# Convolution with residual: the eight VectorE residuals in the middle go the way of the others, and three of four images are combined from image 130

## The chip, the cores and the metric

The kernel runs on one core of one Trainium2 chip. The metric is the device time of one execution in microseconds (us); the median of several executions is compared. TensorE (PE in the profile, its weight loads PEld), VectorE (DVE), ScalarE (ACT), GpSimd (POOL) and SyncE (SP, which issues DMAs) each run their own instructions in order, and wait for each other by semaphores.

## The reference, cut to what matters

```python
# x: (160, 128, 32, 32) f32;  U: (5, 128*128*9) f32
def _gn(v, G=32, eps=1e-5):                  # groups of 4 channels
    g = v.reshape(B_, G, C_ // G, H_, W_)
    m = jnp.mean(g, axis=(2, 3, 4), keepdims=True)
    s = jnp.var(g, axis=(2, 3, 4), keepdims=True)
    return ((g - m) / jnp.sqrt(s + eps)).reshape(v.shape)

s1 = (max(U) - min(U)) / 3.0                 # weights in two quantised parts
v1 = s1 * floor(U / s1)
s2 = s1 / 5.0
v2 = s2 * floor((U - v1) / s2)
w = (v1 + v2).reshape(OUT_CH * 5, IN_CH, 3, 3)
# images 0, 5, 10, ... use weight set 0; 1, 6, 11, ... use set 1; and so on
act = conv(x.reshape(B // 5, 5 * C, H, W), w, padding 1, feature_group_count=5)
out = x + act(_gn(x))                        # the residual
```

Every image is normalised, convolved 3 by 3 with one of five weight sets, and added to its own input.

## The kernel before, in words

The kernel orders the images by weight set: image i of the loop is number `i % 32` of set `i // 32`. One image is a tile of 128 channels by 1024 pixels. Images are loaded in chunks of two (1 MB) into 12 chunk buffers (`CHUNKS`). The order of all instructions is written out by hand in `run` (line 971): iteration i of its loop convolves image i and prepares others at fixed distances.

In iteration i (lines 1103 to 1252), for an image beyond the start:

- **TensorE** (`conv`, 859): first the products m2 and m1 of image i+1 (`sums_of_pairs`, 851), then the main products of image i (`main`, 875) into its pair of PSUM banks, eo. There are two such pairs. The multiplication uses a high and a low f16 part of each image.
- **Two kinds of image.** A *direct* image has a high part hi (`high_part`, ScalarE, 645), a low part lo (VectorE, 748) and three row sums of lo (`combinations`, VectorE, lines 761, 769, 770); it takes 30 matmuls. A *combined* image (`combined`, 648) has its pixels combined in v before the split, by GpSimd (lines 675 and 705) and VectorE (`combine`, 687 and 694), then vh (ScalarE, 735) and vl (VectorE, 741); it takes 24 matmuls. Up to image 29 every second image is combined, then, until `THIRDS` = 146, three of five, and from there three of four.
- **VectorE** in its order: vl or lo and rows of image i+2; a residual by VectorE, if image i-1 has one; eo of image i+1 from m1 and m2 (`pairs`, 897 and 899); v of image i+4 (687 and 694). Steps of the quantisation of the next weight set (lines 134 to 172, by `Later`, 37) are spread between them until four images before the set begins.
- **ScalarE** in its order: the first statistics pass of an image some 14 ahead (241), the copy of the finished image i-1 from PSUM to sum (`residual`, 923), the copy m2 of image i+1 from PSUM to SBUF (`leave`, 888), vh or hi of image i+3, the second statistics pass (248).
- **GpSimd**: the rest of a group's statistics (rstd, line 286), its part of v, or z (711) of image i+4, and an accumulating DMA (`accumulate`, 947). `beside_pairs` and `after` (698, 724) tie the first ones to a VectorE instruction, so that they start at a chosen point.

Statistics are gathered in groups of eight images from image 24 on; the first image of a group, if direct, has its z made by ScalarE (637).

**The residual** has two forms (`residual`, 915). In most images ScalarE copies eo to one of three sum buffers, and GpSimd's queue issues a DMA that adds sum to the output in DRAM (512 KB). The input has been stored there long before (`store_input`, 957), two images in one 1 MB DMA of SP's queue. For images for which `by_hand` (910) is true, VectorE adds eo to the input in its chunk (line 940, one instruction), and SP stores the result (`store`, 955); the other image of that chunk is stored alone. These are images 0 to 2, 39, 55, 71, 87, 103, 119, 135, 151 and 156 to 159.

`by_hand` also sets when a chunk is free for the next load: `consumed` (967) gives iteration i+2 for an image by hand and i-2 for the others. Loads stand in SP's queue in that order, behind the stores.

Of the kernel before, what the change touches and what calls it, by code (L numbers as in the profile page):

```python
# [22 lines left out]
LAST = 4  # L23
# [361 lines left out]
class Main:  # L385
# [27 lines left out]
    STEADY = 7  # L413
    BY_VECTOR = (8, 10, 11, 14, 19, 24, 29, 34)
    FIFTHS = 30
    THIRDS = 146
    EARLY = 8
    FIRST = 3
    HURRIED = (0, 2, 4, 8, 24)
# [228 lines left out]
    def combined(self, i):  # L648
# [4 lines left out]
        if i < self.FIFTHS:  # L653
            return i % 2 == 1
        return i % 5 % 2 == 0 if i < self.THIRDS else i % 4 != 2

# [253 lines left out]
    def by_hand(self, i):  # L910


        return i < self.FIRST or i >= self.imgs - LAST or i > self.FIFTHS and i % 16 == 7

    def residual(self, i):

# [385 lines left out]
```

## Time and profile before

| | |
|---|---|
| median of 3 executions | 975.06 us (974.68 to 976.52) |
| the profiled execution | 975.07 us, its span 973.3 us |
| granted TensorE clock | 0.996 |
| images convolved after the start | 157, from 55 us to 965 us |
| from one VectorE residual in the middle to the next (16 images) | 90 to 93 us |
| residuals by ScalarE's copy and an accumulating DMA | 145 |
| residuals by one VectorE addition of a whole image (line 940) | 13 |
| combined images | 92 |
| DMA queues, share of 16 engines over the span | SP's 46.3%, GpSimd's 42.2% |

The span lies between the first and the last instruction; the time also has what lies around it. Busy time of matmuls is not TensorE at its peak, since matmuls overlap: one follows another after some 0.21 us, although each record lasts about 0.38 us. Idle time that a view shows in brackets is that of the engine just before the instruction, with what ended it. Idle time of an engine that is not on the path costs nothing by itself.

### The profile page before, as it was taken

To read this page: it belongs to the slowest core of one execution; us is meant where nothing else is said; L and a number is where in the kernel's file an instruction comes from. 1 tells how busy PE (TensorE), PEld (TensorE's weight loads), DVE (VectorE), ACT (ScalarE), POOL (GpSimd) and SP (SyncE) were. 2 spreads that over 40 slices of the span, in tenths; PEclk is the share of its full clock that TensorE was granted. 3 is DMA by queue.
4 is the path that set the end of the run, shared out by engine and by line. 5 is a ranking of instruction groups with operands and counts; after the bars stand their busy time and mean duration, and the time that the engine had idled before them with its cause. 6 is when DMAs were issued, how large, how long until landed. Compare 5 with 4: busy or idle time off the path is not lost. (4 is left out here: it accounts for less than half of the span.)

```text
span 973.3 us, 13056 instructions
## 1 busy us (share of the span) xinstructions
PE 930.4 (96%) x4444; PEld 434.5 (45%) x4444; DVE 914.9 (94%) x1290; ACT 854.1 (88%) x1160; POOL 459.3 (47%) x466
## 2 busy tenths in 40 slices
PE   2899999999999999999999999999999999999996
PEld 1344444444444444444444444444444444444443
DVE  7989999999999999989999999999999999988994
ACT  5779999999999999999889999999989999997551
POOL 4345445446335444554355436534444565575550
PEclk9999999999999999999999999999999999999999
DMA  9079999999999997998899899979997999655553
GB/s 352 29 277 345 331 332 322 330 322 318 329 329 337 313 305 217 273 320 229 242 271 319 216 269 298 326 168 298 325 299 158 295 323 229 142 93 92 94 98 112
DMA packets 66427, 250.04 MB, mean 257 GB/s; under 512 B 5296, under 2 KB 5296, under 8 KB 66352
## 3 DMA queue, kind: packets, MB, share of 16 engines
q1 hardware_dynamic: 45472, 173.09, 46.3%
q0 software_dynamic: 20880, 76.03, 42.2%
q8 instruction: 37, 0.61, 0.2%
q14 instruction: 38, 0.31, 0.1%
HBM read 89.19 MB, written 159.91 MB: 256 GB/s over the span
## 5 line engine op out<-in xcount | busy, mean ns | idle before, releaser
L785 PE MATMUL eo<-hi,wt 128*128 128x496 f16 (+3 forms) x1206 | 320.4, 376 | 1.3 <-ACT wt L567 0.7
L840 PEld LDWEIGHTS <-wt 128*128 128x128 f16 x1884 | 183.5, 99 | 213.4 <-DVE rows L770 3.1
L741 DVE SCALAR_TENSOR_TENSOR vl<-v,rstd,vh 128x2048 f16<-128x2048 f32 x92 | 216.8, 2356 | 1.0 <-ACT vh L735 0.9
L840 PE MATMUL eo<-vh,wt 128*128 128x512 f16 x552 | 206.8, 375 | 0.4 <-DVE eo L899 0.2
L840 PE MATMUL eo<-vl,wt 128*128 128x512 f16 x552 | 206.7, 375 | 0.0
L735 ACT ACTIVATE vh<-v,rstd 128x2048 f16<-128x2048 f32 x92 | 184.2, 2002 | 20.5 <-DVE v L694 20.2
L785 PEld LDWEIGHTS <-wt 128*128 128x128 f16 x1278 | 124.7, 99 | 146.7 <-DVE eo L899 4.1
L675 POOL TENSOR_SCALAR v<-xt,ngm 128x64 f32<-128x64 f32 x92 | 85.3, 927 | 219.1 <-issue 63.3
L923 ACT COPY sum<-eo 128x1024 f32<-128x1024 f32 x145 | 152.1, 1049 | 30.6 <-PE eo L840 30.1
L248 ACT ACTIVATE junk<-xt,mv 128x1024 uint8<-128x1024 f32 x152 | 174.5, 1148 | 0.1
L241 ACT ACTIVATE junk<-xt 128x1024 uint8<-128x1024 f32 x152 | 160.5, 1056 | 13.1 <-DMA xt<-in_x_dram 10.0
L711 POOL TENSOR_SCALAR z<-xt,ngm,rstd 128x1024 f32<-128x1024 f32 x50 | 90.1, 1802 | 171.3 <-DVE rows L769 61.0
L840 PEld LDWEIGHTS <-across 128*128 128x128 f16 x1104 | 107.9, 98 | 137.5 <-issue 13.3
L840 PE MATMUL eo<-rows,wt 128*128 128x496 f16 (+1 forms) x390 | 148.1, 380 | 0.0
L947 POOL DMA_DIRECT2D out_dram<-sum x145 | 127.0, 876 | 6.9 <-ACT sum L923 5.8
L888 ACT ACTIVATE m<-m 128x512 f32<-128x512 f32 x157 | 94.0, 598 | 22.1 <-PE m L840 18.1
L840 PE MATMUL m<-vl,across 128*128 128x496 f16 (+1 forms) x276 | 103.3, 374 | 9.4 <-DVE vl L741 9.4
L687 DVE TENSOR_TENSOR v<-xt 128x960 f32<-128x960 f32 x92 | 106.4, 1157 | 0.0
L840 PE MATMUL m<-vh,across 128*128 128x496 f16 (+1 forms) x276 | 103.4, 375 | 0.9 <-ACT m L888 0.9
L705 POOL TENSOR_TENSOR v<-xt 128x512 f32<-128x512 f32 x92 | 95.3, 1036 | 0.0
L748 DVE TENSOR_TENSOR lo<-z,hi 128x1024 f16<-128x1024 f32 x68 | 83.0, 1221 | 0.0
L645 ACT CAST hi<-z 128x1024 f16<-128x1024 f32 x68 | 71.1, 1045 | 0.5
(146 smaller groups left out, 1162.3 us busy)
## 6 DMA issues: line engine op xcount, KB each, us to landing
xt<-in_x_dram SPq DMA_DIRECT2D x78, 1024.0 KB, 12.2
out_dram<-sum POOLq DMA_DIRECT2D x145, 512.0 KB, 8.7
out_dram<-xt SPq DMA_DIRECT2D x68, 1024.0 KB, 17.2
out_dram<-xt SPq DMA_DIRECT2D x23, 512.0 KB, 8.1
u<-in_L_conv_U_dram SPq DMA_DIRECT2D x4, 576.0 KB, 10.6
xt<-in_x_dram SPq DMA_DIRECT2D x4, 512.0 KB, 10.2
range<-in_L_conv_U_dram SPq DMA_DIRECT2D x3, 576.0 KB, 8.3
u<-in_L_conv_U_dram SPq DMA_DIRECT2D x2, 288.0 KB, 3.2
```

The costliest lines, as they stand in the source:

```text
L241: self.nc.scalar.activation(junk, image, ACTF.Copy, scale=-1.0 / image.shape[1], accum_out=self.mv[:, j, 0:1],)
L248: self.nc.scalar.activation(junk, image, ACTF.Square, bias=self.mv[:, j, 0:1], accum_out=self.mv[:, j, 1:2],)
L687: nc.vector.tensor_tensor(self.view(v, 1, (511, 2), (half, H), (1, half - 1)), self.view(x, 1, (1, 2), (W, H), (2, half - 1)), self.view(x ...
L705: ins = nc.gpsimd.tensor_sub(self.v[i][:, 1536:], odd, even)
L711: ins = nc.gpsimd.tensor_scalar(z, self.image(i), st.ngm[:, j], st.rstd[:, j], ALU.add, ALU.mult)
L735: self.nc.scalar.mul(vh, self.v[i], st.rstd[:, j])
L741: yield self.nc.vector.scalar_tensor_tensor(vl, self.v[i], st.rstd[:, j], self.hi[i], ALU.mult, ALU.subtract)
L785: nc.tensor.matmul(self.bank(target, a)[:, first:end, c0:c1], self.wts[n, col][:, k, :], tile[:, s0 : s0 + 2 * (end - first) - 1 : 2, c0 + ...
L840: self.nc.tensor.matmul(out, weights, moving, start=start and j == 0, stop=False, skip_group_check=True)
L888: self.nc.scalar.mul(m2, self.m2_ps, 0.5)
L923: nc.scalar.copy(self.as_banks(i, self.sum[i]), self.flat(i, eo))
L947: added = self.nc.gpsimd.dma_start(self.ov[n, :, b], self.sum.pop(i), accum_op=ALU.add)
```

## The change

`by_hand` loses its third case, so that only the first three and the last four images are added by VectorE. Images 39, 55, 71, 87, 103, 119, 135 and 151 go through ScalarE's copy and the accumulating DMA, their inputs are stored with their neighbours', and their chunks are free four iterations earlier. `THIRDS` goes from 146 to 130: of images 130 to 145, twelve are combined (all but 130, 134, 138 and 142) where ten were (130, 132, 134, 135, 137, 139, 140, 142, 144, 145).

```diff
@@ class Main
     STEADY = 7
     BY_VECTOR = (8, 10, 11, 14, 19, 24, 29, 34)
     FIFTHS = 30
-    THIRDS = 146
+    THIRDS = 130
     EARLY = 8
@@ def by_hand(self, i)
-        return i < self.FIRST or i >= self.imgs - LAST or i > self.FIFTHS and i % 16 == 7
+        return i < self.FIRST or i >= self.imgs - LAST
```

## The prediction

> **What bounds the kernel now.** I read the page first, then the busy times in stretches, then the waits of TensorE, then the timeline around each wait. The page's first part:
>
> ```profile
> PE 930.4 (96%) x4444; PEld 434.5 (45%) x4444; DVE 914.9 (94%) x1290; ACT 854.1 (88%) x1160; POOL 459.3 (47%) x466
> ```
>
> Three engines are nearly full, so the averages decide nothing. The next view has stretches that each run from one VectorE residual in the middle to the next, 16 images (columns: length, busy PE, PEld, DVE, ACT, POOL, then clock, DMA share, GB/s):
>
> ```profile
> 284.20:376.50 92.30, 92.25 (x445) 43.16 (x443) 90.74 (x128) 89.72 (x124) 41.09 (x42) 1.00 1.00 295
> 376.50:469.40 92.90, 90.91 (x434) 42.29 (x433) 88.37 (x121) 84.92 (x115) 44.01 (x44) 1.00 0.93 265
> 653.20:746.00 92.80, 89.89 (x432) 41.53 (x431) 90.56 (x123) 86.40 (x121) 42.85 (x43) 1.00 0.93 264
> 746.00:836.10 90.10, 90.10 (x434) 42.30 (x433) 83.39 (x114) 86.52 (x117) 48.40 (x42) 1.00 0.95 265
> 836.10:927.00 90.90, 89.92 (x430) 42.07 (x429) 81.98 (x101) 70.55 (x87) 52.84 (x45) 1.00 0.60 105
> ```
>
> The reader is to see that 16 images take some 90 us where TensorE never waits (746 to 836), and 92 to 93 us where VectorE also quantises the next weight set. So TensorE's own work bounds the kernel, plus the times at which VectorE is late. Those times are few after image 30, and each stands in TensorE's timeline (the bracket is idle time and its releaser):
>
> ```profile
> 383.32 0.38 PE L840 MATMUL m<-vl,across 128*128 128x512 f16 x1 [1.05 <-DVE vl L741]
> 469.30 0.38 PE L840 MATMUL m<-vl,across 128*128 128x512 f16 x1 [0.66 <-DVE vl L741]
> 472.28 0.39 PE L785 MATMUL eo<-hi,wt 128*128 128x512 f16 x1 [0.50 <-DVE eo L899]
> 500.55 0.38 PE L840 MATMUL m<-vl,across 128*128 128x512 f16 x1 [1.95 <-DVE vl L741]
> 684.23 0.60 PE L840 MATMUL m<-rows,wt 128*128 128x512 f16 x2 [0.87 <-DVE rows L770]
> 730.40 0.38 PE L840 MATMUL m<-vl,across 128*128 128x512 f16 x1 [1.95 <-DVE vl L741]
> 911.20 0.38 PE L840 MATMUL m<-vl,across 128*128 128x512 f16 x1 [0.98 <-DVE vl L741]
> 933.85 0.38 PE L840 MATMUL m<-vl,across 128*128 128x512 f16 x1 [0.87 <-DVE vl L741]
> ```
>
> Matmuls follow each other every 0.21 us although a record lasts 0.38, so a wait costs about 0.16 more than its bracket: 381.90 to 383.32 is 1.42 from start to start, 1.21 of it lost. The eight cost 8.83 + 8 x 0.16 = 10.1 us.
>
> **What the Trainium skill says.** Perfetto Trace Analysis, "Identifying the Most-Contended Engine": matmul busy time is no measure of TensorE's limit; occupancy is one for VectorE and ScalarE. The 0.38 and 0.21 agree, which is why I count starts. SBUF — State Buffer, "Who interferes with whom": a VectorE instruction with two SBUF inputs and a GpSimd instruction that reads SBUF exclude each other. The trace agrees: L309 takes 0.17 us alone and 0.96 beside L705 (906.18), L675 takes 0.4 alone and 2.3 beside a vl. The residual addition has one PSUM and one SBUF input, so removing it should free no GpSimd time. ScalarE: Activation LUTs, "What ACT_TABLE_LOAD costs": back-to-back ACTIVATEs overlap by about 93 ns; here a copy of 1.05 us holds ScalarE 0.97 from start to start (701.75 to 702.72). DMA: Bandwidth & Descriptors, "Issuing engines are not separate DMA queues": all DMAs share 16 engines, so the added accumulating stores compete with loads wherever they are issued.
>
> **The change part by part.** Costs are from these rows:
>
> ```profile
> L940 DVE TENSOR_TENSOR xt<-eo,xt 128x1024 f32<-128x1024 f32 x13 | 15.8, 1218 | 4.7 <-PE eo L840 3.6 <-PE eo L785 1.0
> L923 ACT COPY sum<-eo 128x1024 f32<-128x1024 f32 x145 | 152.1, 1049 | 30.6 <-PE eo L840 30.1
> L947 POOL DMA_DIRECT2D out_dram<-sum x145 | 127.0, 876 | 6.9 <-ACT sum L923 5.8 <-DMA out_dram<-xt 1.1
> ```
>
> *1. Eight additions leave VectorE* (images 39, 55, 71, 87, 103, 119, 135, 151). Each held it 1.35 us from its start to the next start (284.23 to 285.58): 8 x 1.35 = 10.8 us. This is worth only what a TensorE wait behind it was worth, before VectorE next has time to spare. Image by image: 39 (284.2) and 55 (376.5) precede the wait at 383.32, with VectorE never waiting between; 1.21 goes. 71 (469.4) precedes 472.28: 471.41 to 472.28 less 0.21 is 0.66, gone. The wait at 469.30 lies ahead of that addition and stays. VectorE then waits 1.02 us for ScalarE at 482.89, which uses up the rest of the lead, so 500.55 stays. 87 (562.4): VectorE waits at 600.83, 617.57 and 628.99, TensorE not until 684; nothing. 103 (653.2): no VectorE wait over 0.25 before 684.23, so that goes: 1.04. What is left of the lead ends at 712.75 (0.74 waiting for ScalarE), so 730.40 stays. 119 and 135: TensorE doesn't wait behind them; nothing. 151 (927.0): the wait at 933.85 goes, 1.04. Sum: 1.21 + 0.66 + 1.04 + 1.04 = 3.95 us.
>
> *2. Eight copies go to ScalarE*, 0.97 each, 7.8 us, ahead of the copy m2 (L888) in its queue, for which VectorE's L897 waits, and ahead of vh or hi and the second statistics pass. What hides them is the wait that ScalarE has right behind each of these images now:
>
> ```profile
> 288.83 2.00 ACT L735 ACTIVATE vh<-v,rstd 128x2048 f16<-128x2048 f32 x1 [1.35 <-DVE v L694]
> 381.11 2.00 ACT L735 ACTIVATE vh<-v,rstd 128x2048 f16<-128x2048 f32 x1 [1.58 <-DVE v L694]
> 467.08 2.00 ACT L735 ACTIVATE vh<-v,rstd 128x2048 f16<-128x2048 f32 x1 [1.21 <-DVE v L694]
> 650.85 0.60 ACT L888 ACTIVATE m<-m 128x512 f32<-128x512 f32 x1 [2.31 <-PE m L840]
> 750.64 2.00 ACT L735 ACTIVATE vh<-v,rstd 128x2048 f16<-128x2048 f32 x1 [1.27 <-DVE v L694]
> 839.46 1.02 ACT L923 COPY sum<-eo 128x1024 f32<-128x1024 f32 x1 [1.08 <-PE eo L840]
> ```
>
> Image 87 has three short ones (0.58, 0.26, 0.34 from 564.76), and 151 has 1.27 at 928.97. At 39 the copy moves m2 from 282.19 to 283.16, still ahead of VectorE, which comes to L897 at 284.23 without the addition. Where v released ScalarE, v comes 1.35 earlier as well. Cost 0; with that cover gone, 7.8.
>
> *3. DMA and queues.* Eight more accumulating stores: GpSimd 8 x 0.88 = 7 us (it is 47% busy, and the issue stands behind the work VectorE needs); on the DMA engines 42.2% x 973.3 / 145 = 2.83 us each, 23 us in all, where the shares of the page (46.3 + 42.2 + 0.4) leave 108 idle. A store lands a median 8.7 us after issue (12.4 at most), and three sum buffers last about 3 x 5.8 = 17 us, so ScalarE shouldn't wait. On SP the late store of each of these images goes; the queue stood behind it (292.3 us in 12 waits), and the chunk is freed four iterations earlier. No engine waited for a load after 80 us, so this is worth 0. Bounds: no gain, since nobody waits; at worst, landings slow enough to hold sum buffers, put at 1 us for each of the eight stores, which the range covers in part.
>
> *4. Two more combined images.* In 130 to 145 there are 12 for 10. A combined one costs TensorE 2.54 + 2.55 us (390.88 to 393.42, 379.35 to 381.90), a direct one 1.29 + 5.11 (372.70 to 379.10): 1.31 less, 2.6 for two. VectorE takes on 2 x 1.5 us and has 95.87 of 107.30 busy at 774.7 to 882.0. ScalarE, start to start: statistics 2.32, sum 0.97, m2 0.48, and vh 1.90 or hi 0.93, so 5.67 or 4.70; 12 x 5.67 + 4 x 4.70 + 0.3 = 87.1 us for 16 images, against TensorE's 12 x 5.09 + 4 x 6.40 + 0.6 = 87.3 (0.3 and 0.6 are the small steps of two groups' statistics). (Image 136 no longer needs ScalarE's z, 1.24.) It just fits.
>
> What is late next: groups that begin at a combined image. At 152, rstd (L286) starts only behind rows of the direct image before it, VectorE waits, L309 meets GpSimd, and TensorE loses 909.84 to 911.20 less 0.21 = 1.15 us. The new mix gives 136 and 144 the same neighbours (134 and 142 direct): 2 x 1.15 = 2.3. Part 4 is worth 2.6 - 2.3 = 0.3; from -1.6, if they are like the waits at 500.55 and 730.40 (2.1 each, which also open a group), to 2.6.
>
> Sum: 3.95 + 0.3 = 4.2 us. The profiled execution took 975.07 (span 973.3 and 1.8 around it), the median is 975.06; 975.07 - 4.2 = **970.9 us**.
>
> **Rivals.** *The waits move (22%)*: freed VectorE time is used up by the next ScalarE wait more often than I found, half of 3.95 stays, and part 4 costs 1.6: 975.07 - 2.0 + 1.6 = 974.7. For it: VectorE already waits for m2 in 3.6 us of 284 to 770. Against: at 383 and 684 nothing stands between.
> *ScalarE becomes the bound, slower (18%)*: place: m2 behind the new copy, then L897, then TensorE; price 0.97 per image, 7.8: 975.07 + 7.8 - 4.2 = 978.7. It decides once ScalarE's waits of a stretch fall under 0.97; 284 to 376 has 2.6 us left, and the measuring part of 130 to 145 almost none. Against: the six waits above.
> *VectorE's whole lead counts (15%)*: all waits but that of 152 go: 10.1 - 1.15 = 8.95, and 0.3: 965.8.
>
> **How the numbers follow.** Forecast 45%. A measurement tells about 0.2% (1.95 us) from no change, so faster means under 973.1 and slower over 977.0. Faster is 0.43 of the forecast and the third rival's 0.15, together 0.58; within is the first rival's 0.22, 0.02 of the forecast's upper edge and 0.01 of the second rival, 0.25; slower is the second's other 0.17. The range 967.0 to 977.5 reaches into the outer rivals and leaves out about 2 in 10. Most chance has one sign.
>
> **What would show it.** L940 x5 and L923 x153. Right: the TensorE waits near 383, 472, 684 and 933 gone, those near 469, 500 and 730 still there, about 4 us earlier at the end; new waits of about 1 us ahead of the groups at 136 and 144; ScalarE's waits behind the eight images filled. Wrong: VectorE waiting for m (L888) more than now, TensorE waiting for eo (L899), ScalarE waiting for a DMA at L923, or a stretch of 16 images above 93 us.

## The result and the profile after

The changed kernel took 969.27 us (969.01 to 969.63), beside 974.87 us for the kernel before on the same chip: a ratio of 0.9944, with a 95% interval of 0.9932 to 0.9955. That is 5.6 us less (4.4 to 6.6 by the interval), and the forecast was 4.2 less than the profiled execution of before. Ratios below are likewise to the kernel before on the same chip. The profiled execution of after took 969.63 us, its span 967.9.

The first part of the page of after, against the one of before in the prediction:

```profile
PE 925.9 (96%) x4432; PEld 433.3 (45%) x4432; DVE 911.0 (94%) x1280; ACT 861.9 (89%) x1167; POOL 462.9 (48%) x477
```

TensorE has 12 matmuls fewer (two combined images instead of two direct ones), ScalarE 7.8 us more work, VectorE 3.9 less: eight additions of 1.22 us went, and the two combined images and other steps gave part of it back. The totals say no more about the time than they did before. The rows of the three operations that the change touches, in the view of groups that keeps shapes apart:

```profile
L940 DVE TENSOR_TENSOR xt<-eo,xt 128x1024 f32<-128x1024 f32 x5 | 6.1, 1219 | 3.6 <-PE eo L840 3.6
...
L923 ACT COPY sum<-eo 128x1024 f32<-128x1024 f32 x153 | 160.5, 1049 | 28.7 <-PE eo L840 28.0
L947 POOL DMA_DIRECT2D out_dram<-sum x153 | 133.7, 876 | 11.7 <-ACT sum L923 5.4 <-DMA out_dram<-xt 3.6 <-ACT m L888 1.8
```

Eight moved as the diff says, at unchanged durations; no wait of L923 for a DMA stands in its row. The same stretches of 16 images as in the prediction, now bounded by VectorE's step L897 of the image two places later (41, 57, 73, 105, 121, 137, 153), because the addition that bounded them is gone:

```profile
283.50:375.40 91.90, 91.90 (x445) 43.22 (x443) 89.72 (x128) 90.65 (x124) 41.90 (x43) 1.00 1.04 322
375.40:467.00 91.60, 90.72 (x435) 42.39 (x434) 87.21 (x121) 86.30 (x118) 44.74 (x45) 1.00 1.02 293
...
650.20:741.70 91.50, 89.55 (x432) 41.60 (x431) 89.39 (x122) 86.21 (x121) 42.97 (x44) 1.00 1.00 273
741.70:833.00 91.30, 90.32 (x434) 42.36 (x433) 84.51 (x111) 87.87 (x117) 48.46 (x45) 1.00 0.97 257
833.00:922.30 89.30, 87.37 (x418) 40.81 (x416) 83.14 (x99) 73.27 (x89) 53.02 (x47) 1.00 0.60 95
```

The second and third row are 1.3 us shorter than before, and each held one of the waits that were to go (383, 684). The last is 1.6 us shorter for another reason: it has 12 matmuls fewer (418 for 430), some 2.6 us, and one new wait. The fourth row, where TensorE never waited, is 1.2 us longer at the same 434 matmuls; TensorE's busy time is now 1.0 below its length, so a wait has appeared in it. All TensorE waits of more than 0.5 us for VectorE's vl after image 30, in the timeline of TensorE of after:

```profile
466.86 0.38 PE L840 MATMUL m<-vl,across 128*128 128x512 f16 x1 [0.68 <-DVE vl L741]
...
497.44 0.38 PE L840 MATMUL m<-vl,across 128*128 128x512 f16 x1 [1.95 <-DVE vl L741]
...
726.11 0.38 PE L840 MATMUL m<-vl,across 128*128 128x512 f16 x1 [1.95 <-DVE vl L741]
...
817.21 0.38 PE L840 MATMUL m<-vl,across 128*128 128x512 f16 x1 [0.98 <-DVE vl L741]
...
861.85 0.38 PE L840 MATMUL m<-vl,across 128*128 128x512 f16 x1 [0.96 <-DVE vl L741]
...
906.50 0.38 PE L840 MATMUL m<-vl,across 128*128 128x512 f16 x1 [0.97 <-DVE vl L741]
```

The four waits that were to go (383, 472, 684, 933) are gone. The three that were to stay (469, 500, 730) stand at the same images with the same sizes. Two new ones, at 817 and 862, stand ahead of the groups at 136 and 144, and the one of the group at 152 stays. ScalarE, in its timeline of after, at the places where the prediction showed its waits:

```profile
286.19 1.08 ACT L923 COPY sum<-eo 128x1024 f32<-128x1024 f32 x1
287.16 0.59 ACT L888 ACTIVATE m<-m 128x512 f32<-128x512 f32 x1
287.64 2.00 ACT L735 ACTIVATE vh<-v,rstd 128x2048 f16<-128x2048 f32 x1
...
378.59 2.00 ACT L735 ACTIVATE vh<-v,rstd 128x2048 f16<-128x2048 f32 x1
...
464.64 2.00 ACT L735 ACTIVATE vh<-v,rstd 128x2048 f16<-128x2048 f32 x1 [0.75 <-DVE v L694]
```

The waits of 1.35 and 1.58 us ahead of the first two vh are filled, and of 1.21 at the third 0.75 is left. Of the signs that the prediction named for being wrong none came: no stretch of 16 images takes more than 92.2 us, and VectorE waits less for m, not more. From the view of waits, over the whole execution (us in total, times, longest), before and then after:

```profile
DVE eo L897 <- ACT m L888: 12.9, 15, 1.4
```

```profile
DVE eo L897 <- ACT m L888: 7.6, 8, 1.4
```

To see where the time went, I lined up both traces by image: how much earlier TensorE starts the first product, m2, of an image than in the profiled execution of before.

| at image | lead, us | what lies between |
|---|---|---|
| 36 | 0.73 | nothing of the change yet |
| 52 | 1.00 | 39 |
| 60 | 2.46 | 55, the wait of 383 |
| 76 | 3.11 | 71, the wait of 472 |
| 104 | 3.15 | 87 |
| 112 | 4.31 | 103, the wait of 684 |
| 128 | 4.29 | 119 |
| 146 | 4.69 | 135, and the new mix |
| 156 to 159 | 5.73 | 151, the wait of 933 |

The first 0.73 is not the change: up to image 36 the engines do the same work in both programs, and only SP's stores of two inputs (39 and 55) differ. The eleven kernels below led by 0.0 to 1.5 us there, and six of these programs have nothing that sets them apart from after up to that image. So the change itself is worth 5.73 - 0.73 = 5.0 us. The profiled times differ by 5.4; the other 0.3 is lost behind the last product. In the kernels below that differ from after only further on or in lacking the copies, each step of the table up to image 76 repeats within 0.03 us; only that of 103 varies, from 1.13 to 1.36.

### The profile page after: what moved, and what is told of

Its sections match the earlier page's. It is cut to its first block, busy times and chain, and to the rows that moved or that the text cites. A ratio compares the mean times of both kernels' runs of the same rounds, so it can differ in the third digit from the quotient of the medians.

```text
span 967.9 us, 13056 instructions
## 1 busy us (share of the span) xinstructions
PE 925.9 (96%) x4432; PEld 433.3 (45%) x4432; DVE 911.0 (94%) x1280; ACT 861.9 (89%) x1167; POOL 462.9 (48%) x477
## 4 chain that ended last, share of the span: by engine, by line
PE 65%; DVE 12%; ACT 3%; issue 3%; POOL 2%; POOLq 0%; DVEq 0%; ACTq 0%
PE eo L840 22%; PE eo L785 18%; PE m L840 12%; PE m1b L840 6%; PE m1a L840 6%; DVE vl L741 3%; DVE v L687 2%; POOL rstd L286 1%; ACT vh L735 1%; DVE v L694 1%; DVE lo L748 1%; DVE eo L897 1%; ACT junk L248 1%; DVE eo L899 1%; ACT junk L241 0%
## 5 line engine op out<-in xcount | busy, mean ns | idle before, releaser
L785 PE MATMUL eo<-hi,wt 128*128 128x496 f16 (+3 forms) x1170 | 310.3, 375 | 0.7 <-ACT wt L567 0.7
L840 PEld LDWEIGHTS <-wt 128*128 128x128 f16 x1884 | 183.8, 99 | 211.8 <-DVE eo L899 1.7
L741 DVE SCALAR_TENSOR_TENSOR vl<-v,rstd,vh 128x2048 f16<-128x2048 f32 x94 | 221.5, 2357 | 1.0 <-ACT vh L735 0.9
L840 PE MATMUL eo<-vh,wt 128*128 128x512 f16 x564 | 211.3, 375 | 0.2 <-DVE eo L899 0.2
L840 PE MATMUL eo<-vl,wt 128*128 128x512 f16 x564 | 211.2, 375 | 0.0
L735 ACT ACTIVATE vh<-v,rstd 128x2048 f16<-128x2048 f32 x94 | 188.1, 2001 | 13.1 <-DVE v L694 12.9
L923 ACT COPY sum<-eo 128x1024 f32<-128x1024 f32 x153 | 160.5, 1049 | 28.7 <-PE eo L840 28.0
L785 PEld LDWEIGHTS <-wt 128*128 128x128 f16 x1242 | 120.9, 99 | 140.2 <-DVE eo L899 2.4
L840 PE MATMUL eo<-rows,wt 128*128 128x512 f16 x378 | 143.5, 380 | 0.0
L947 POOL DMA_DIRECT2D out_dram<-sum x153 | 133.7, 876 | 11.7 <-ACT sum L923 5.4
L687 DVE TENSOR_TENSOR v<-xt 128x960 f32<-128x960 f32 x94 | 109.7, 1167 | 0.0
L286 POOL TENSOR_TENSOR rstd<-ve,mhalf 128x8 f32<-128x8 f32 (+2 forms) x24 | 41.2, 1717 | 67.2 <-DVE rows L769 22.0
## 6 DMA issues: line engine op xcount, KB each, us to landing
out_dram<-xt SPq DMA_DIRECT2D x76, 1024.0 KB, 19.6
```

Of the source, the lines that this page charges most:

```text
L687: nc.vector.tensor_tensor(self.view(v, 1, (511, 2), (half, H), (1, half - 1)), self.view(x, 1, (1, 2), (W, H), (2, half - 1)), self.view(x ...
L735: self.nc.scalar.mul(vh, self.v[i], st.rstd[:, j])
L741: yield self.nc.vector.scalar_tensor_tensor(vl, self.v[i], st.rstd[:, j], self.hi[i], ALU.mult, ALU.subtract)
L785: nc.tensor.matmul(self.bank(target, a)[:, first:end, c0:c1], self.wts[n, col][:, k, :], tile[:, s0 : s0 + 2 * (end - first) - 1 : 2, c0 + ...
L840: self.nc.tensor.matmul(out, weights, moving, start=start and j == 0, stop=False, skip_group_check=True)
L923: nc.scalar.copy(self.as_banks(i, self.sum[i]), self.flat(i, eo))
```

## The experiments

Two theories stood against each other: the time is the sum of the TensorE waits behind removed additions, and copies and stores are hidden (the prediction's); or one of the two halves, or the copies, does something else. Leads below are those of the table, less the lead at image 36.

**Each half alone.** On the changed kernel, the old mix of images:

```diff
-    THIRDS = 130
+    THIRDS = 146
```

> Only the first half of the change: no image in the middle is added by VectorE, three of four images are combined from image 146 as before. My theory (four TensorE waits behind the additions of 55, 71, 103 and 151 go, the copies cost nothing): the waits near 383, 472, 684 and 933 are gone, those near 469, 500, 730 and 911 stay; about 970 us (974.9 less some 4.5 to 5). Rival 'ScalarE has no room': over 974. Rival 'the gain came from the combined images': 974 or more.

Measured: 969.75 us (969.46 to 970.6), ratio 0.9953 (0.9936 to 0.9969). Its trace gains 4.81 us from image 36 on, and the waits at 467, 497 and 726 are those of after. So the residuals alone are nearly the whole gain. (The 4.81 is more than their 4.6 in the table mostly because the step of 103 is 1.36 here.) The other half alone, on the kernel before:

```diff
-    THIRDS = 146
+    THIRDS = 130
```

> Only the second half: three of four combined from image 130, VectorE still adds the eight images. My theory: two times 1.31 us less on TensorE, given back by waits ahead of the groups at 136 and 144 (about 1.1 each) and, with the addition of 135 on a VectorE that has less room, perhaps one more of about 1; so 974 to 975.5. Rival 'the fewer matmuls count in full': 972.3, with no new TensorE waits between 800 and 880.

Measured: 975.03 us (974.51 to 975.65), ratio 1.0005 (0.9996 to 1.0013). Between images 130 and 146 it loses 0.6 us against before, although it has 12 matmuls fewer. (Between 36 and 116, where the two programs are the same, its lead drifts by 0.3, so a smaller difference over a long stretch tells nothing.) TensorE's timeline of this kernel shows why:

```profile
820.90 0.38 PE L840 MATMUL m<-vl,across 128*128 128x512 f16 x1 [0.97 <-DVE vl L741]
...
843.57 0.38 PE L840 MATMUL m<-vl,across 128*128 128x512 f16 x1 [0.89 <-DVE vl L741]
...
866.59 0.38 PE L840 MATMUL m<-vl,across 128*128 128x512 f16 x1 [0.96 <-DVE vl L741]
```

The first and third are the waits of the groups at 136 and 144, as forecast. The middle one is not in the prediction, which put 135 at nothing; the expectation above had it as a "perhaps". It stands behind the addition of image 135, which cost nothing in the old mix. The sum of the halves (4.8 - 0.6 = 4.2) is 0.8 short of the change's 5.0, near the 0.89 + 0.16 of this one wait: with both halves made, the addition of 135 isn't there to cause it.

**Additions that were priced at nothing.** On the changed kernel, three additions back on VectorE:

```diff
-        return i < self.FIRST or i >= self.imgs - LAST
+        return i < self.FIRST or i >= self.imgs - LAST or i in (87, 119, 135)
```

> The changed kernel with the VectorE additions of images 87, 119 and 135 kept. My theory: at 87 and 119 the addition lies where VectorE has time to spare before TensorE next waits, so they cost nothing; 135 now lies where three of four are combined and may cost up to 1 us. 969.3 to 970.3, with no new TensorE wait behind 562 and 746. Rival 'each addition costs its 1.35 us': 973.3.

Measured: 970.37 us (970.22 to 971.07), ratio 0.9961 (0.9947 to 0.9975), just above the range expected. Between 540 and 800 us TensorE has only the wait of 726, as in after: 87 and 119 cost nothing. At 135 the lead of TensorE falls by 1.03 us between images 138 and 140, at this line of its timeline:

```profile
840.00 0.38 PE L840 MATMUL m<-vl,across 128*128 128x512 f16 x1 [0.87 <-DVE vl L741]
```

So "135: nothing" holds for the old mix and fails in the new one.

**Copies and stores.** On the changed kernel, the eight images get neither addition, copy nor accumulating DMA; the convolution of these images is missing from the output:

```diff
     def residual(self, i):
...
+        if i > self.FIFTHS and i % 16 == 7 and i < self.imgs - LAST:
+            return
```

> The changed kernel, in which the eight images of the middle get neither VectorE's addition nor ScalarE's copy and accumulating DMA: their convolution is left out of the output, all else is done. It prices the copies and DMAs. My theory (they fill waits that ScalarE has anyway, and nobody waits for the DMAs): within 0.5 us of the changed kernel, 968.8 to 969.8. Rival 'the copies cost their 0.97 us where ScalarE is full': up to 7.8 us less, 961.5.

Measured: 969.76 us (969.07 to 969.99), ratio 0.9949 (0.9932 to 0.9966); from image 36 on it gains 4.94 us, beside 5.00 in after. So without the eight copies and eight accumulating stores the kernel is no faster: together they cost nothing that this can tell. (The earlier release of the chunks was not tried by itself; in neither trace does one of the four compute engines wait for a load after 190 us.) Where that cover ends was tried by making the copy twice in these images:

```diff
+            if i > self.FIFTHS and i % 16 == 7:
+                nc.scalar.copy(self.as_banks(i, self.sum[i]), self.flat(i, eo))
```

> The changed kernel with ScalarE's copy made twice for the eight images, the second time over the first: 0.97 us more on ScalarE each, nothing else. It finds the edge of the cover. My theory: the copy uses up most of the wait behind each image, and TensorE has over 2 us between m2 and the main products, so the second copy costs less than half of its 7.8 us: 969.5 to 972.5. Rival 'ScalarE was at its edge already': 977.

Measured: 971.73 us (971.22 to 972.11), ratio 0.9969 (0.9958 to 0.9981): 2.5 us by medians, 1.9 by the traces, as expected less than half of what the second copies take. That is rather more than the 7.8 assumed: at image 39 the two copies hold ScalarE 1.11 and 0.98 us from start to start, where a single one takes 0.97, and over the eight images m2 is delayed by some 8.7 us. Between 270 and 880 us VectorE's waits for m come to 8.1 us in 13 waits, beside 4.6 in 5 in after. VectorE's timeline of this kernel at image 39, and then the same in after:

```profile
282.98 0.35 DVE L146 TENSOR_TENSOR k<-nnn,lt 128x384 f16<-128x384 int16 x1
283.94 0.70 DVE L897 SCALAR_TENSOR_TENSOR eo<-m1b,m 128x512 f32<-128x512 f32 x1 [0.60 <-ACT m L888]
```

```profile
283.27 0.35 DVE L146 TENSOR_TENSOR k<-nnn,lt 128x384 f16<-128x384 int16 x1
283.54 0.69 DVE L897 SCALAR_TENSOR_TENSOR eo<-m1b,m 128x512 f32<-128x512 f32 x1
```

The second copy delays m2 by 1.1 here, and VectorE waits 0.60 of it: at this image one copy was covered with some 0.4 to 0.5 us to spare. This is the way by which the rival "ScalarE becomes the bound" would have come about; it opens with the second copy and not with the first.

**The waits ahead of the groups.** The prediction laid them to rstd, which waits for the rows of the direct image two places ahead of the group. Two other orders of the same mix, on the changed kernel. First, direct images at `i % 4 == 3`, so that none stands two ahead of a group:

```diff
-        return i % 5 % 2 == 0 if i < self.THIRDS else i % 4 != 2
+        return i % 5 % 2 == 0 if i < self.THIRDS else i % 4 != (3 if i < 156 else 2)
```

> The changed kernel with the direct images of the last part at 131, 135, ... 151, 155 instead of 130, 134, ... 150, 154 (158 stays direct): as many combined images, but the image two before each group's start (134, 142, 150) is combined. My theory (the waits at 817, 862 and 906 come because rstd of the group starts only behind the rows of that direct image): the three are gone or under 0.3, some 3 us less: 966 to 967. Rival 'VectorE is simply full where three of four are combined, the group's small steps cost 1.4 us wherever they lie': waits of the same sum at other places, 969 to 970.

Measured: 966.59 us (965.97 to 966.79), ratio 0.9917 (0.9900 to 0.9933). TensorE has no wait for VectorE left after 780 us, which the rival "VectorE is simply full" did not allow. Second, each group starts with a direct image:

```diff
-        return i % 5 % 2 == 0 if i < self.THIRDS else i % 4 != 2
+        return i % 5 % 2 == 0 if i < self.THIRDS else i % 4 != 0 and i != 158
```

> The changed kernel with the direct images of the last part at 132, 136, ... 156 and 158: as many combined images, but each group (136, 144, 152) starts with a direct one, whose normalisation is ScalarE's (1.24 us each) and needs no v from VectorE behind rstd. My theory: the three waits are gone, 966 to 967.5. Rival 'ScalarE has no room for 1.24 more where it also measures': its vh and m2 come late, TensorE waits instead, 969 or more.

Measured: 968.13 us (967.59 to 968.46), ratio 0.9930 (0.9911 to 0.9946), less than expected. Of the three waits of about 1 us, two of 0.6 are left, at 849 and 894 us; ahead of each VectorE had waited for ScalarE (0.36 for m at 838, 0.46 for vh and 0.36 for m from 879 on), as the rival had it, though at a smaller price. Both orders agree with the cause, and only the first removes the waits.

**The cause itself.** rstd (L286) need not start behind rows; the program ties it there with `after`. On the changed kernel, without the tie:

```diff
-                        self.after(st.power(), before)
+                        st.power()
```

> The changed kernel with GpSimd's rstd (L286) of each group not tied to a VectorE instruction any more: it starts as soon as ScalarE's ve is there. My theory: VectorE's L307 no longer waits for it, L309 no longer meets L705 (0.17 instead of 0.96), so VectorE is some 1.1 us earlier at each group: the waits at 817, 862 and 906 go (about 3.3), those at 497 and 726 fall from 1.95 to about 0.9; 964 to 966. Rival 'the tie is there because rstd beside a VectorE instruction with two inputs holds that up': rstd takes 2.8 to 3.6 us, VectorE loses as much elsewhere, 968 to 971.

Measured: 962.26 us (961.83 to 962.98), ratio 0.9872 (0.9856 to 0.9889): better than expected, 7.0 us under the changed kernel, and no version tried is clearly faster. The rival (968 to 971) is refuted. The timelines of GpSimd and VectorE ahead of the group at 136, first in after, then in this kernel:

```profile
810.05 1.71 POOL L286 TENSOR_TENSOR rstd<-ve,mhalf 128x8 f32<-128x8 f32 x1 [5.92 <-DVE rows L769]
...
810.87 0.70 DVE L899 SCALAR_TENSOR_TENSOR eo<-m1b,m 128x512 f32<-128x512 f32 x1
...
811.79 0.37 DVE L307 TENSOR_SCALAR rstd<-rstd,lift 128x8 f32<-128x8 f32 x1 [0.22 <-POOL rstd L286]
812.20 0.96 DVE L309 TENSOR_TENSOR shift<-ngm,rstd 128x8 f32<-128x8 f32 x1
813.08 1.15 DVE L687 TENSOR_TENSOR v<-xt 128x960 f32<-128x960 f32 x1
```

```profile
803.00 2.00 POOL L286 TENSOR_TENSOR rstd<-ve,mhalf 128x8 f32<-128x8 f32 x1 [2.43 <-ACT ve L279]
...
807.92 0.22 DVE L307 TENSOR_SCALAR rstd<-rstd,lift 128x8 f32<-128x8 f32 x1
808.17 0.17 DVE L309 TENSOR_TENSOR shift<-ngm,rstd 128x8 f32<-128x8 f32 x1
808.25 1.15 DVE L687 TENSOR_TENSOR v<-xt 128x960 f32<-128x960 f32 x1
```

In after, GpSimd stood idle for 5.92 us, and then VectorE waited for rstd and met GpSimd in L309: from the start of L307 to that of L687 it took 1.29 us. Without the tie this is 0.33, rstd having ended some three microseconds before L307. How much of the saving is rstd's wait and how much the meeting in L309 was not tried apart: by these lines 0.79 of it is L309's length. The waits of TensorE for vl between 270 and 970 us, in the view of waits (line waited for, us in total, times, longest), again after and then this kernel:

```profile
PE m L840 <- DVE vl L741: 7.7, 7, 2.0
```

```profile
PE m L840 <- DVE vl L741: 1.8, 3, 0.7
```

The two waits of 1.95 us, which the change left alone, came mostly from the same tie: they are 0.70 and 0.71 here. How much the change is worth when the tie is gone was tried on the kernel before, with the same edit:

> The kernel before (eight additions by VectorE, three of four combined from 146) with only rstd not tied. It asks whether the eight additions still cost anything once VectorE is earlier at each group. My theory (an addition costs only what TensorE waits behind it): VectorE gains 1.1 us at each group, so the waits behind 55, 71 and 103 shrink or go, that behind 151 stays in part; the difference to the changed kernel with rstd untied (962.3) falls from 5.0 to 1 to 3 us: 963.5 to 965.5. Rival 'the two gains add up': 967.2.

Measured: 968.09 us (967.66 to 968.72), ratio 0.9932 (0.9915 to 0.9948). My theory missed it: the difference is 5.8 us, not 1 to 3, and the plain sum of the two gains (967.2) came nearer. TensorE's waits for VectorE in this kernel, between 270 and 970 us:

```profile
PE m L840 <- DVE vl L741: 3.5, 5, 0.9
PE eo L785 <- DVE eo L899: 0.5, 1, 0.5
PE m L840 <- DVE rows L770: 0.2, 1, 0.2
```

The wait for rows, that of 684, has shrunk from 0.87 to 0.2. Image by image against the changed kernel without the tie, the residuals are worth 3.3 us here: 55 costs 1.03 (1.46 with the tie), 103 0.60 (1.16), and 71 and 151 what they cost before. So here the theory had the direction. But between 130 and 146 the combined images now count 2.66 us, the full 2 x 1.31 of the forecast's part 4, because nothing gives it back. I had left that half out of the expectation. That the two gains nearly add up is thus chance: one part shrinks by 1.3 us without the tie, the other grows by 2.3.

**More combined images.** With the tie gone, still more images can be combined, from 120 on, and then, in the second kernel, seven of eight from 146 on:

```diff
-    THIRDS = 130
+    THIRDS = 120
```

```diff
-        return i % 5 % 2 == 0 if i < self.THIRDS else i % 4 != 2
+        return i % 5 % 2 == 0 if i < self.THIRDS else i % (4 if i < 146 else 8) != 2
```

> The changed kernel with rstd not tied and three of four combined from image 120 on (eight of 120 to 129 instead of six). My theory: VectorE has no weights to quantise from about 124 on and now waits for TensorE there, so the 12 matmuls less count nearly in full: 962.3 - 2.6 = 959.7, up to 961 if the statistics fill ScalarE. Rival 'ScalarE (5.67 us for a combined image against TensorE's 5.09) becomes the bound': 962 or more, VectorE waiting for m from ScalarE and TensorE for eo.

> As the one with three of four from 120, and seven of eight from 146 (150 and 158 combined too). No statistics are measured from there, so ScalarE has room, and VectorE waits some 1.4 us of every four images for TensorE in the changed kernel with rstd untied. My theory: 2.6 us less again than with three of four from 120: 957 to 958. Rival 'VectorE is late at once where six images in a row are combined (5.5 us against TensorE's 5.09)': waits for vl come back, 959 or more.

Measured: 962.02 us (961.6 to 962.77), ratio 0.9868 (0.9852 to 0.9885), which can't be told from the kernel without these combined images; and 963.94 us (963.46 to 964.5), ratio 0.9888 (0.9871 to 0.9904). Both miss their expectations (959.7 to 961, and 957 to 958). In the first, TensorE's waits for vl between 270 and 970 us are, beside the 1.8 us in 3 waits without these images:

```profile
PE m L840 <- DVE vl L741: 4.1, 5, 1.3
```

The two new ones, 1.05 and 1.29 us at 746 and 769, give the 12 matmuls back: with 0.16 each they are 2.66. VectorE still prepares the next weights there (L145 and L146 ahead of the first, L571 to L573 ahead of the second), which the expectation had ended too early. The time is that of the ScalarE rival, its mechanism is not: between 715 and 775 us VectorE never waits for m. In the second, the view of waits from 880 to 970 us shows VectorE late, in part behind ScalarE:

```profile
DVE vl L741 <- ACT vh L735: 2.9, 4, 1.4
PE m L840 <- DVE vl L741: 2.4, 4, 1.1
```

Of VectorE's four waits for vh only two, 0.65 and 0.21 us at 893 and 909, stand ahead of these waits of TensorE. VectorE is late often enough here that the fewer matmuls no longer pay.

## Why the prediction was right

| step | forecast, us | measured in the table of leads |
|---|---|---|
| additions 39 and 55, wait of 383 | 1.21 | 1.46, and 0.27 ahead of image 52 |
| 71, wait of 472 | 0.66 | 0.65 |
| 87 | 0 | 0.04 |
| 103, wait of 684 | 1.04 | 1.16 |
| 119 | 0 | -0.02 |
| 135 and two more combined images | 0.3 | 0.40 |
| 151, wait of 933 | 1.04 | 1.04 |
| sum | 4.2 | 5.0 |

*Part 1* was right by place and by mechanism: a removed addition of 1.35 us was worth the TensorE wait behind it, not its own length, and 10.8 us of VectorE work gave 4.6 us in this table and 4.8 in the kernel with the residuals alone. The sum was 0.8 too small. Most of that is the term of 39 and 55, by some 0.5 us: I counted only the wait at 383 and passed over delays below a quarter of a microsecond ahead of it. The wait of 467, ahead of the addition of 71, stayed, and so did 497 and 726, ahead of which the lead was to be used up. At 497 the trace shows how: VectorE's wait for ScalarE's wt at 480 grew from 1.02 to 1.25 us, with a new one of 0.36 for TensorE's m1b just before it. That these three kept their sizes refutes "VectorE's whole lead counts", and that the four waits are gone refutes "the waits move".

*Parts 2 and 3* were right: 0, by the kernel with neither copy nor store. One reading was not quite so: in before GpSimd does wait for a load after 80 us, once, 2.85 us at 187.6. That is ahead of image 39, and after has the same wait. The margin was thinner than the 1.2 to 2.3 us of the listed waits made it look: the second copies together cost 1.9 to 2.5 us. ScalarE's wait was for v or the product, but m2 stands ahead of it in the queue, and at image 39 its due time at L897 left only some 0.4 to 0.5 us. The price of 7.8 "with the cover gone" was not reached even so. The ScalarE rival was wrong for one copy per image; with two its path begins to show, at about a quarter of what the copies take.

*Part 4* was right in both terms: 2.66 us of matmuls (shown where nothing gives them back) and two new waits of 0.98 and 0.96 us in brackets, 1.14 and 1.12 lost, for 1.15 forecast; without the tie they are gone, as the reason given for them asks. What it missed is the tie to part 1: in the new mix the addition of 135 would have cost 1.03, so the parts could not be priced one by one. Here that made no difference to the sum, because both were changed together.

The forecast missed the median by 1.6 us, within its range: 0.8 is the sum above, and the rest is not laid to the change by the leads: single executions start differently by as much.

## What to carry to other kernels

Price work that is taken from an engine which isn't the bound by the bounding engine's wait behind it, before the first engine next waits for a third; everything else of it is slack that someone uses up. Ask of each wait that stays what released the releaser: here an ordering written out by hand cost about 7 us, more than the change gained, and it also hid the worth of the combined images (0.4 us with it, 2.66 without). Price edits that touch the same stretch together, since one may open the wait that the other closes.

## What was not expected of the hardware

- A small VectorE step beside GpSimd: L309 on 128 x 8 took 0.17 us at 808 in the kernel without the tie and 0.96 in after, where it met GpSimd's combining step. The prediction had this from the Trainium skill, SBUF — State Buffer, "Who interferes with whom". New is that a longer GpSimd step is harmless if it is early: without the tie the median of rstd rose from 1.71 to 2.10 us (4.0 at most), and VectorE's 13 waits for it (2.9 us) are gone.
- The start of the same program differs by up to 1.5 us from execution to execution at image 36, as much as the largest single step that is priced here. Leads by image separate this from a change; two total times don't.
- With eight more accumulating stores the DMA share stood at 1.00 to 1.04 in the first five of the stretches of 16 images (322 GB/s in the first). The accumulating stores landed a median 8.8 us after issue, beside 8.7 before, the input stores of 1 MB 19.6 beside 17.2. In these stretches no wait of TensorE, VectorE, ScalarE or GpSimd for a DMA stands in the trace of after.
